# Two-layer decoder on one core: in the last entry's attention with heads of 64, the routed rows' transposes and the first piece of the shared expert go ahead of the denominators' last sums

## The chip, the cores and the metric

The kernel runs on one core of one Trainium2 chip. The metric is the device time of one execution in microseconds (us), the median of several runs. Five runs of the kernel before gave 1140.53 to 1144.34 us, median 1142.88.

The engines are named as the profile names them: PE is TensorE (matmuls and transposes), PEld its weight loads, DVE is VectorE, ACT ScalarE, POOL GpSimd, and SP the SyncE queue that issues most DMAs.

## The reference, cut to what matters

The program is a decoder of two layers on `x` of 8 entries by 256 tokens by 256 dimensions, all in float32. Layer 0 has self-attention, cross-attention and a routed feed-forward part; layer 1 has causal self-attention, cross-attention with 16 heads of 64, and experts. The change lies where the last two meet:

```python
# L1 cross-attention, context (8, 256, 512), one null key and value in front
q = q * scale
sim = jnp.einsum('bhid,bhjd->bhij', q, k)
attn = jax.nn.softmax(sim, axis=-1)
out = jnp.einsum('bhij,bhjd->bhid', attn, v)
out = jnp.einsum('bnf,fd->bnd', out, Wout)
out = layernorm(out) * ln_scale + ln_bias
...
# L1 experts: one of 8 per token, and a shared one for all tokens
x_aD = layernorm(x).reshape(2048, 256)
scores_aE = x_aD @ router_DE              # the best expert's score gives the gate
shared_aD = jax.nn.silu(x_aD @ ws1_DF) * (x_aD @ ws3_DF) @ ws2_FD     # F = 704
```

The softmax needs, per head and query, the sum of the exponentials over the keys (the denominator). The shared expert needs nothing but the normalized rows of the tokens that it is applied to.

## The kernel before, in words

**The cross-attention with heads of 64** (`null_cross_attention`) is a loop over the 8 entries. The 16 heads stand as 8 pairs `c`; a pair's 128 rows are its two heads of 64. For each pair, `weighted` (called once per entry) does the following:

- TensorE makes the scores `stx` of both heads and both halves of the keys (line 1554), ScalarE their exponentials `pTx` (line 1558), and GpSimd adds the two halves of the keys into `both` (line 1560).
- TensorE multiplies exponentials and values into `ox` (line 1594), two pairs to a PSUM tile. The result goes to `oT` in SBUF, undivided, by ScalarE for pairs 0, 1, 4, 5 and by VectorE for pairs 2, 3, 6, 7 (line 1602).
- `sums` (line 1569) sums `both` over its partitions with a small matmul against a column of ones, `hot8`, into one PSUM tile `den` of 128 by 256, two matmuls per pair. The sums of a block of two pairs are issued one block later; those of the last block, pairs 6 and 7, are left to `rest()`, which the loop calls where it likes.

Then `reciprocals` (lines 1611 to 1636) adds the null key's exponential `en` to `den` and takes the reciprocal `r` on VectorE (lines 1614 and 1615). It sends `r` to DRAM as `rd` with four DMAs on SP (line 1621) and back as `rs`, spread over 64 partitions each, with two more (line 1625). Beside that, GpSimd forms `en * r`, and two VectorE operations test the range of `r` (lines 1631, 1632). `divide` (line 1649) multiplies `oT` by `rs` in four parts of two pairs; in the last entry GpSimd does the first and third, VectorE the second and fourth. `outward` (line 1653) makes the product with `Wout` in seven smaller products (the tiles `wo` and `woz`) from blocks of `oT` and their sums and differences `swo` (lines 1463 to 1466, VectorE), then norms the result and adds it to `x`. Between its sixth and its seventh product it runs one step of other work, `between`.

**What fills the gap in the last entry.** In the first seven entries the next entry's keys, values and queries are made while `rs` is under way. The last entry has no next one, so pieces of the shared expert take their place. `hidden_shared(0, ...)` (lines 1191 to 1200, over `hidden`, line 1178) is a generator over six pieces of the first quarter of the tokens (512 of 2048, entries 0 and 1). A whole piece is four matmuls of 128 by 128 by 512 into a pair of PSUM banks `hx` (line 1196), which the profile shows as eight rows, each matmul of the program twice; then a silu on ScalarE into `spx` (line 1188) and a product with the other bank on VectorE into `mid` (line 1189). The sixth piece is a half one. The pairs for `hx` come from a pool with two buffers. Four pieces run between the reciprocals and `divide`, the fifth within `outward`, the sixth behind it.

In the same place stand the routed rows: `routed_rows(b - 1, ...)` (line 1316) transposes the normalized rows of entry 6 with four TensorE transposes (line 287, tile `tr`, three PSUM buffers shared with `ox`) into `xnTe`, copied by ScalarE; `routed_scores(b - 1)` (line 1331) makes their router scores `sc` behind the first piece.

**What sets the order.** From the point where `order.enter_context(tc.manual_schedule(...PE...))` stands, TensorE runs in the order in which the program is written. The other engines' queues are put in order by the framework's scheduler, from its own estimate of when things are ready. Every engine then works through its queue in order and waits on semaphores.

So the last entry's order on TensorE is: last `ox`, last `den` sums, `tr`, piece 1, `sc`, pieces 2 to 4, `outward`. On VectorE, ahead of the last two copies of `ox`, stand sums of the shared weights (`tws`, line 1208) and of rows (`sx`, lines 1220 to 1223); behind the copies come `rx` and its reciprocal, the two range tests, the copy of `sc`, three `mid` products, the two divides, the first `swo` sum, the fourth `mid` product and the other `swo` sums.

Of the kernel before, what the change touches and what calls it, by code (L numbers as in the profile page):

```python
# [157 lines left out]
def plain(  # L158
# [101 lines left out]
    def layernorm_T(b, work, mm, bufs=2):  # L260

        xn = work.tile([P, 2, D], F32, tag="xn", name="xn", bufs=bufs)
        mv, rs = norm_stats([x[:, 2 * b + t, :] for t in range(2)], 1e-5, small, "ln")
        for t in range(2):
            last = normed(xn[:, t, :], x[:, 2 * b + t, :], mv, rs, t)
        return last, transposed(xn, work, mm, "xnT", bufs=bufs)
# [308 lines left out]
    first = ExitStack()  # L575
# [315 lines left out]
    def context(b):  # L891
        t = ctxs.tile([P, CTX // P, S], F32, tag="ctxT", name="ctxT")
        nc.sync.dma_start(t, a["ctx_T"][b].rearrange("(c p) t -> p c t", p=P))
        return t

    def key_room():
        return kvs.tile([P, nc8, S], F32, tag="kT", name="kTx")
# [280 lines left out]
    def hidden(mid, first, n, pair, silu):  # L1178

        for i in range(NFC):  # L1180
            h1, h3 = pair(n)
            for h, lo in ((h1, i * P), (h3, FF + tail + i * P))[: 2 if i < full else 1]:
                first(h, lo)
            fw = P
            if i == full:
                fw, h1, h3 = tail, h1[:tail], h1[tail:]
            sl = silu(n)[:fw]
            nc.scalar.activation(sl, h1, AF.Silu)  # L1188
            yield nc.vector.tensor_tensor(mid[:fw, i, :n], sl, h3, ALU.mult)  # L1189

    def hidden_shared(q, pair, silu):


        def first(h, lo):
            for c in range(2):
                nc.tensor.matmul(
                    h, shared["ws13"][:, c, lo : lo + P], shared["xnT"][:, c, bass.ts(q, 2 * S)], start=c == 0, stop=c == 1
                )

        return hidden(shared["mid_s"][q % 2], first, 2 * S, pair, silu)  # L1200
# [105 lines left out]
    def routed_norm(b, work):  # L1306

        xn = work.tile([P, 2, D], F32, tag="y", name="xne", bufs=1)
        mv, rs = norm_stats([x[:, 2 * b + t, :] for t in range(2)], 1e-5, small, "ln")
        for kept, v in zip(norms[b], (mv, rs)):  # L1310
            nc.gpsimd.tensor_copy(kept, v)
        for t in range(2):
            normed(xn[:, t, :], x[:, 2 * b + t, :], mv, rs, t)
        return xn

    def routed_rows(b, xn, work):
        if b < B - 2:
            rows_of[b] = transposed(xn, work, mm, "xnk", bufs=1)
            nc.sync.dma_start(xt[b], rows_of[b])
        else:  # L1320
            rows_of[b] = transposed(xn, work, mm, "", shared["xnT"][:, :, bass.ts(b, S)])
# [87 lines left out]
    def null_cross_attention(phase):  # L1409
# [44 lines left out]
        def sums_of_rows(rows, n, name, apart, pool=wsum):  # L1454


            def block(i, j):
                return rows[:, n * j : n * (j + 1), bass.ts(i, P)]

            sw = pool.tile([P, 4 if apart else 3, n, P], F32, tag=name, name=name, bufs=1)  # L1460
            s1, s2, s4 = (sw[:, i] for i in range(3))
            s3 = sw[:, 3] if apart else block(1, 0)
            nc.vector.tensor_tensor(s1, block(1, 0), block(1, 1), ALU.add)
            nc.vector.tensor_tensor(s2, s1, block(0, 0), ALU.subtract)
            nc.vector.tensor_tensor(s4, block(0, 1), s2, ALU.subtract)
            nc.vector.tensor_tensor(s3, block(0, 0), block(1, 0), ALU.subtract)
            return block(0, 0), block(0, 1), s4, block(1, 1), s1, s2, s3
# [143 lines left out]
        def reciprocals(b, den, en):  # L1611

            r = work.tile([P, S], F32, tag="rx", name="rx", bufs=1)
            nc.vector.tensor_tensor(r, den, en, ALU.add)
            nc.vector.reciprocal(r, r)
            rd = dram.tile([2, nc8, S], F32, name=f"rd{b}")
            rs = work.tile([P, nc8, S], F32, tag="rs", name="rs", bufs=1)
            for g in range(2):
                for i in range(2):
                    at = XD * g + HP * i  # L1620
                    nc.sync.dma_start(
                        rd[g].rearrange("(c i) q -> i c q", i=2)[i], r[at : at + nc8 // 2, :]
                    )
            for g in range(2):
                nc.sync.dma_start(
                    rs[XD * g : XD * (g + 1)].rearrange("p c q -> p (c q)"),
                    rd[g : g + 1].rearrange("g c q -> g (c q)").to_broadcast([XD, nc8 * S]),
                )
            nc.gpsimd.tensor_tensor(en, en, r, ALU.mult)
            low = work.tile([P, S], F32, tag="low", name="low", bufs=1)  # L1630
            nc.vector.tensor_scalar(low, r, 1.0e-25, None, ALU.is_ge)
            nc.vector.scalar_tensor_tensor(
                low, r, 1.0e25, low, ALU.is_le, ALU.mult, accum_out=fit[:, b : b + 1]
            )
            return rs
# [75 lines left out]
        def spare():  # L1711
            return work.tile([P, 2, 2 * S], F32, tag="pT", name="spx", bufs=4)
# [20 lines left out]
        for b in range(B):  # L1733
            more = b + 1 < B
            if more:
                ctxT = context(b + 1)
            oT, den, rest = weighted(kT, v, qT)
            if more:
                _, xnT = layernorm_T(b + 1, work, mm, 1)
                if b:  # L1740
                    xe = routed_norm(b - 1, work)
                of_ctx = sums_of_rows(ctxT, CTX // P // 2, "sw", False)
            else:
                xe = routed_norm(b - 1, work)
                rest()

                wproj.close()
                late = ctx.enter_context(tc.tile_pool(name="late", bufs=1, side="right"))
                load_shared(late, lambda: ctx.enter_context(tc.tile_pool(name="mids", bufs=1, side="right")))
                tables = ctx.enter_context(tc.tile_pool(name="route", bufs=1, side="right"))  # L1750
                sums = phase.enter_context(tc.tile_pool(name="sums", bufs=1, side="right"))
                order.enter_context(tc.manual_schedule(engines={mybir.EngineType.PE}))
            if more:
                order.enter_context(tc.manual_schedule(engines={mybir.EngineType.PE}))
            if b:
                routed_rows(b - 1, xe, work)
            if more:
                of_x = sums_of_rows(xnT, 1, "swq", True)
                kT, v, qT = key_room(), value_room(), query_room()
                k7 = seven("k7", of_ctx, w_terms(kv_blocks, 0), kT, False)  # L1760
                v7 = seven("v7", of_ctx, w_terms(kv_blocks, 1), v, True)
                q7 = seven("q7", of_x, w_terms(q_blocks, 0), qT, False)
                next(k7)
                rest()
            rs, old = reciprocals(b, den, en), en
            if not b:
                sums_of_weights(o_blocks, slice(0, 4))
            if b == 1:
                in_range()
            if not more:  # L1770
                w_out(shared["ws2"], a["L1_ffn_ws2_FD"])
                routing_tables(tables)
            if more:

                for made in (k7, k7, v7, k7, k7, k7, v7, v7, q7, v7, q7, v7, v7, q7):
                    next(made)
            else:
                first = hidden_shared(0, pair, lambda n: spare()[:, 0, :n])
                for i in range(4):
                    next(first)  # L1780
                    if i == 0:
                        routed_scores(b - 1)
                shared["of_w"] = sums_of_shared(*(sums.tile([P, full * P], F32, name=f"tws{i}") for i in range(4)))
            divide(oT, rs, (nc.gpsimd, nc.gpsimd if more else nc.vector))
            outward(b, oT, old, lambda: next(q7 if more else first))
            if more:
                next(q7)
                if b:
                    routed_scores(b - 1)
                next(q7)  # L1790
                en = null_key(xnT)
            else:
                for _ in first:
                    pass
            order.close()
# [1230 lines left out]
```

## Time and profile before, and how to read it

| | before |
|---|---|
| median of 5 runs | 1142.88 us (1140.53 to 1144.34) |
| profiled execution, its own time | 1144.87 us |
| its span, first to last instruction | 1143.1 us |
| TensorE matmuls busy | 1093.1 us, 96% |
| TensorE weight loads busy | 715.8 us, 63% |
| VectorE, ScalarE, GpSimd busy | 52%, 40%, 38% |
| mean granted TensorE clock | 0.990 |
| last entry's end of attention | about 855 to 897 us of the span |

The trace has, for every instruction, its start, its duration, and the idle time of its engine just before it, with the engine, the tile and the line that ended that idle time. A row of the timeline can merge several like instructions; the count at its end says how many, and its duration then runs from the first start to the last end. Matmul ends are modelled, and rows on GpSimd are rough. The granted clock is the share of TensorE's full speed that its throttle allowed.

### The profile page before, as it was taken

Reading aid. Unit: us, or ns where it says so; the run is one execution under the profiler, and the core shown is the slowest. Engines: PE = TensorE matmul, PEld = TensorE weight load, DVE = VectorE, ACT = ScalarE, POOL = GpSimd, SP = SyncE. Lnnn points to the kernel's source line nnn. Section 1 sums busy time; section 2 is a strip of 40 time slices with the busy share of each in tenths; the row PEclk is TensorE's granted clock in tenths of the full one; section 3 lists DMA queues with packets and bytes.
Section 4 is the critical chain, followed back from the end, with each engine's and each line's share of the span. In section 5 each row is a group of like instructions: output and inputs, shape, how many; then the busy total and the mean of one; then the engine's idle time right before and its main releaser. Section 6 shows DMA issues by size and latency. Waiting matters only on the chain. (4 is left out here: it accounts for less than half of the span.)

```text
span 1143.1 us, 34931 instructions
## 1 busy us (share of the span) xinstructions
PE 1093.1 (96%) x15186; PEld 715.8 (63%) x15186; DVE 591.6 (52%) x1573; ACT 460.9 (40%) x747; POOL 439.4 (38%) x519
## 2 busy tenths in 40 slices
PE   6999999989899999999999999999999999999996
PEld 3444545544544545777777777777775768888864
DVE  5576776778686628344434352525257672222213
ACT  4776766665454533232323232323233321322220
POOL 2456364547587623433242424242425133000023
PEclk9999999999899999999999999999999999999999
DMA  8048344134033400101010101010122045999924
GB/s 261 5 159 283 100 133 124 58 124 133 30 124 102 187 2 20 39 20 48 20 49 20 48 20 48 20 48 20 48 103 69 1 159 200 369 414 397 372 70 128
DMA packets 62819, 130.87 MB, mean 114 GB/s; under 512 B 9904, under 2 KB 45984, under 8 KB 58304
## 3 DMA queue, kind: packets, MB, share of 16 engines
q1 hardware_dynamic: 54944, 108.61, 27.9%
q0 software_dynamic: 4992, 16.92, 4.1%
q10 hardware_dynamic: 2720, 3.02, 0.8%
q8 instruction: 121, 1.98, 0.7%
q14 instruction: 42, 0.34, 0.1%
HBM read 110.03 MB, written 35.80 MB: 128 GB/s over the span
## 5 line engine op out<-in xcount | busy, mean ns | idle before, releaser
L341 ACT ACTIVATE pT<-st 128x1024 f32<-128x1024 f32 (+1 forms) x128 | 110.5, 916 | 64.7 <-PE st L330 58.8
L367 PE MATMUL o<-pT,padv 128*32 128x256 f32 (+1 forms) x1536 | 96.6, 367 | 1.6 <-DVE by_q L383 1.1
L1560 POOL TENSOR_TENSOR both<-pTx 128x512 f32<-128x512 f32 x64 | 87.4, 1395 | 21.0 <-ACT pTx L1558 19.1
L272 PE MATMUL h<-xrT,w 128*64 128x128 f32 (+1 forms) x1936 | 87.1, 250 | 0.7 <-issue 0.7
L272 PEld LDWEIGHTS h<-xrT,w 128*64 128x64 f32 x1936 | 84.5, 137 | 3.7 <-issue 1.3
L341 ACT ACTIVATE pT<-st,kbias 128x1024 f32<-128x1024 f32 x64 | 67.9, 1113 | 36.8 <-PE st L330 34.8
L1189 DVE TENSOR_TENSOR midr<-sl,h 128x128 f32<-128x128 f32 x102 | 29.4, 288 | 101.3 <-PE h L272 68.8
L367 PEld LDWEIGHTS o<-pT,padv 128*32 128x32 f32 x1536 | 44.6, 110 | 53.4 <-issue 23.8
L1558 ACT ACTIVATE pTx<-stx 128x1024 f32<-128x1024 f32 x64 | 62.5, 1024 | 31.4 <-PE stx L1554 28.1
L1188 ACT ACTIVATE sl<-h 128x128 f32<-128x128 f32 (+1 forms) x114 | 35.4, 311 | 94.9 <-PE h L272 55.9
L330 PE MATMUL st<-qm,kT 32*128 32x512 f32 (+1 forms) x512 | 68.6, 594 | 4.9 <-ACT qm L309 1.9
L278 PE MATMUL qk<-xnT,l_wqkv 128*32 128x256 f32 x1024 | 69.0, 396 | 0.6 <-issue 0.6
L1554 PE MATMUL stx<-qTx,kTx 64*128 64x256 f32 x512 | 64.4, 391 | 2.1 <-ACT pTx L1558 2.1
L1594 PE MATMUL ox<-pTx,vx 128*32 128x256 f32 x1024 | 63.3, 380 | 0.0
L383 DVE STREAM_TRANSPOSE by_q<-o 128x512 f32<-128x512 f32 x48 | 34.1, 710 | 51.2 <-PE o L367 51.1
L1649 POOL TENSOR_TENSOR oT<-oT,rs 128x512 f32<-128x512 f32 x30 | 37.2, 1271 | 60.3 <-DMA rs<-rd 60.3
L1554 PEld LDWEIGHTS stx<-qTx,kTx 64*128 64x128 f32 x512 | 46.1, 186 | 20.4 <-issue 7.0
L346 POOL TENSOR_SCALAR_AFFINE_SELECT pT<-pT 128x512 f32<-128x512 f32 x64 | 41.9, 672 | 35.6 <-ACT pT L341 34.9
L254 POOL TENSOR_TENSOR lxrs<-lxve,mhalf 128x2 f32<-128x2 f32 x8 | 5.7, 706 | 129.4 <-DVE lxve L252 129.4
L278 PEld LDWEIGHTS qk<-xnT,l_wqkv 128*32 128x32 f32 x1024 | 34.2, 114 | 28.8 <-issue 9.3
L2014 PE MATMUL out<-w,midr 128*64 128x256 f32 x408 | 47.6, 379 | 1.0 <-issue 1.0
L1594 PEld LDWEIGHTS ox<-pTx,vx 128*32 128x32 f32 x1024 | 35.3, 110 | 21.1 <-issue 2.7
(397 smaller groups left out, 2225.3 us busy)
## 6 DMA issues: line engine op xcount, KB each, us to landing
w<-packs SPq DMA_DIRECT2D x22, 1408.0 KB
w<-packs SPq DMA_DIRECT2D x22, 768.0 KB
rs<-rd SPq DMA_DIRECT2D x16, 512.0 KB
packs<-L_ffn_w_eDF SPq DMA_DIRECT2D x8, 704.0 KB
packs<-L_ffn_w_eDF SPq DMA_DIRECT2D x8, 640.0 KB
packs<-L_ffn_w_eFD SPq DMA_DIRECT2D x8, 640.0 KB
ctxT<-ctx_T SPq DMA_DIRECT2D x8, 512.0 KB
wkv_x<-L_xattn_Wkv POOLq DMA_DIRECT2D x1, 4096.0 KB
```

Source lines behind the costliest of these rows:

```text
L272: nc.tensor.matmul(out[h], lhsT[:, h], rhs, start=start, stop=stop, skip_group_check=True)
L278: nc.tensor.matmul(out[h : h + HP], lhsT[:, h : h + HP], rhs, start=start, stop=stop, skip_group_check=True)
L330: nc.tensor.matmul(st[:, r, :, :n], self.kT[rows, c, bass.ts(kt, P)], self.qm[rows, :, c, q0:], start=True, stop=True,)
L341: nc.scalar.activation(pT[:, :, :, :n], st[:, 2 * k : 2 * k + 2, :, :n], AF.Exp, scale=self.scale, **kb)
L346: nc.gpsimd.affine_select(out=pT[:, :, :, :P], in_=pT[:, :, :, :P], compare_op=ALU.is_ge, fill=0.0, base=0, pattern=[[0, 2], [0, 2], [1, P ...
L367: nc.tensor.matmul(o[HP * j : HP * j + HP, m, q0:], self.v_pad[:, kt, 8 * c + 2 * j + m, :], pTs[j // 2][:, j % 2, m, : S - q0], start=kt ...
L1554: nc.tensor.matmul(st[:, g, kt, :], kT[rows, c, bass.ts(kt, P)], qT[rows, c, :], start=True, stop=True)
L1558: nc.scalar.activation(pT, st, AF.Exp, scale=scale)
L1560: nc.gpsimd.tensor_tensor(both, pT[:, :, 0, :], pT[:, :, 1, :], ALU.add)
L1594: nc.tensor.matmul(o[at : at + HP, i, :], v[:, kt, 2 * (c2 + i) + g, lo : lo + HP], pT[:, g, kt, :], start=kt == 0, stop=kt == 1, skip_gro ...
L1649: engines[c2 % 4 // 2].tensor_tensor(oT[:, c2 : c2 + 2, :], oT[:, c2 : c2 + 2, :], rs[:, c2 : c2 + 2, :], ALU.mult)
L2014: nc.tensor.matmul(ps[h], mid[:, i, h], sets[k % len(sets)][1][:, i, :], start=i == 0, stop=i == NFC - 1, skip_group_check=True,)
```

## The change

In the last entry, `rest()` (the sums of pairs 6 and 7) moves from ahead of the closing of pools and the loads of the shared expert's weights to behind the routed rows' transposes and behind the first step of `hidden_shared`. The generator is therefore made earlier, and the later loop takes three steps of it instead of four; `routed_scores` stands behind the first of these, which is now the second piece. Nothing else of the program differs; the pools, the loads and the arithmetic are the same.

```diff
@@ -1742,7 +1742,6 @@
                 of_ctx = sums_of_rows(ctxT, CTX // P // 2, "sw", False)
             else:
                 xe = routed_norm(b - 1, work)
-                rest()
 
                 wproj.close()
                 late = ctx.enter_context(tc.tile_pool(name="late", bufs=1, side="right"))
@@ -1762,6 +1761,10 @@
                 q7 = seven("q7", of_x, w_terms(q_blocks, 0), qT, False)
                 next(k7)
                 rest()
+            if not more:
+                first = hidden_shared(0, pair, lambda n: spare()[:, 0, :n])
+                next(first)
+                rest()
             rs, old = reciprocals(b, den, en), en
             if not b:
                 sums_of_weights(o_blocks, slice(0, 4))
@@ -1775,8 +1778,7 @@
                 for made in (k7, k7, v7, k7, k7, k7, v7, v7, q7, v7, q7, v7, v7, q7):
                     next(made)
             else:
-                first = hidden_shared(0, pair, lambda n: spare()[:, 0, :n])
-                for i in range(4):
+                for i in range(3):
                     next(first)
                     if i == 0:
                         routed_scores(b - 1)
```

## The prediction

> **What bounds the kernel now.** I read the page first. Its busy row says that TensorE's matmuls fill the span, so a step is worth what it does to TensorE's own queue, and any moment in which TensorE stands still behind 868 us is paid in full unless a later stall swallows it.
>
> ```profile
> PE 1093.1 (96%) x15186; PEld 715.8 (63%) x15186; DVE 591.6 (52%) x1573; ACT 460.9 (40%) x747; POOL 439.4 (38%) x519
> ```
>
> The chain of waits on the page is no help: it holds three pieces of the last microsecond. So I went on to the list of waits, for TensorE alone. From 889 us to the end it stood still five times, 0.2 to 1.0 us each, 3.1 us in all, and each time for another engine that had itself been fed by TensorE (or for nothing that shows). None of these is a wait for something with a clock of its own, so nothing behind the place of the change gives a delay back.
>
> Then the timeline of the place itself. Columns: start, duration, engine, line and operation, count, and in brackets the idle time before and who ended it.
>
> ```profile
> 867.11 0.39 PE L1594 MATMUL ox<-pTx,vx 128*32 128x256 f32 x2
> ...
> 867.98 0.62 PE L1569 MATMUL den<-both,hot 128*32 128x256 f32 x4 [0.45 <-POOL both L1560]
> 868.12 1.27 DVE L1602 COPY oT<-ox 128x512 f32<-128x512 f32 x2
> 868.86 0.66 PE L287 MATMUL tr<-ident,xne 128*128 128x128 f32 x4 [0.26 <-DVE oT L1602]
> 869.32 0.41 DVE L1614 TENSOR_TENSOR rx<-den,en 128x256 f32<-128x256 f32 x1
> 869.35 3.60 PE L1196 MATMUL hx<-xnTe,ws 128*128 128x512 f32 x8
> 869.77 1.75 DVE L1615 RECIPROCAL rx<-rx 128x256 f32<-128x256 f32 x1
> ...
> 872.88 0.64 PE L272 MATMUL sc<-router,xnTe 128*64 128x8 f32 x16
> ...
> 873.45 10.57 PE L1196 MATMUL hx<-xnTe,ws 128*128 128x512 f32 x24
> ...
> 880.59 2.49 POOL L1649 TENSOR_TENSOR oT<-oT,rs 128x512 f32<-128x512 f32 x2 [7.57 <-DMA rs<-rd]
> 881.92 2.31 DVE L1649 TENSOR_TENSOR oT<-oT,rs 128x512 f32<-128x512 f32 x2
> ...
> 883.95 1.09 PE L272 MATMUL wo<-wout_x,oT 128*64 128x128 f32 x16
> ```
>
> The reader is to see two things. TensorE stands still around the last `den` sums twice, 0.45 us for GpSimd's last `both` and 0.26 us for VectorE's late copy of `ox`, 0.71 us together. And from those sums a second chain runs: `rx`, reciprocal, out to DRAM and back, divide, outward product. That chain comes home just in time: VectorE's first divide ends near 883.6 (it began at 881.92; the two of them take 0.68 and 1.71 us by their rows), and the product `wo` that needs it starts at 883.95, directly behind the last `hx`. The margin is about 0.3 us, and four pieces of the shared expert, 14 us, are what covers the chain.
>
> **The change, part by part.** No instruction is added or removed; in the built streams only the queues of TensorE and VectorE change their order, those of ScalarE, GpSimd and SP do not. TensorE's `den` matmuls move behind the four transposes and the first piece. VectorE's first `mid` product moves ahead of the two range tests, and the fourth moves ahead of the divides.
>
> *The stall in front.* The transposes do not come sooner: they write the PSUM buffer that VectorE's first late copy frees (868.12 + 0.63 = 868.75), and the copies stand behind the weight sums in VectorE's queue, which the change leaves alone. So `tr` starts at 868.86 as before and TensorE is idle from 867.52 (867.12 + 0.40, the end of what runs with the last `ox`) to there, 1.34 us. The sums, which lay inside that wait, now cost their own time behind the first piece: two full rounds of eight rows, at 858.34 and 862.57, each held TensorE 0.46 and 0.45 us until the next product. So **+0.46 us** (below 0.3 seems excluded, the rows being real work; 0.7 if the change of tile form costs something, though `hx` to `sc` and back shows no gap). What was meant to fill a wait fills none, since another wait of the same length lay behind it.
>
> *The chain behind.* One piece takes 872.88 - 869.35 = 3.53 us, so `den` now starts at 872.88. `rx` followed the start of `den` by 0.70 to 0.71 us in four earlier entries (466.64 to 467.35, 523.87 to 524.57, 581.63 to 582.34, 754.95 to 755.65), so it starts at 873.58 instead of 869.32, 4.26 us later. VectorE idles meanwhile; behind `rx` wait only the `mid` products, whose PSUM pairs are needed again two pieces later. Sum and reciprocal end 2.20 us on, at 875.78. From the reciprocal's end to GpSimd's first divide the eight entries show 8.53 to 9.76 us, this one 9.07: SP's six DMAs (four out, two back, nothing queued behind them there) are the same. The first divide can start at 884.85 and ends at 886.12 (1.27 us).
>
> *TensorE's side.* It reaches `wo` at 883.95 + 0.46 = 884.41, behind three pieces instead of four since `den`. VectorE must first do the fourth `mid`: silu starts 0.17 us after the matmuls (884.12 against 883.95) and takes 0.60, the product follows 0.03 us later with 0.69, so VectorE is free at 885.90. Its first divide then waits for GpSimd's running one, as VectorE's 881.92 row did in before (1.71 us beside GpSimd's second, 0.68 alone): 886.12 + 0.69 = 886.8. `wo` starts near 886.9 instead of 884.41. GpSimd's second divide runs 886.8 to 888.05, VectorE's second to 888.65, and the second half of `woz`, in before at 885.31 (884.87 plus half of 0.88), starts at 888.7: 3.4 us late. The sums `swo` behind it keep ahead of their products. With the longest of the eight round trips it is 4.1 us, with the shortest VectorE comes second to GpSimd and it is still 3.5; if VectorE got its turn at once, 2.9. I take **+3.4 us in all, the 0.46 included**: about 3.0 us of standing still, 2.5 of it in one piece.
>
> *The clock.* Between its first and its last matmul the kernel runs at full granted clock but for four times before 302 us. Cut at the edges of those times, the span falls into a raster of 3.41 us. Columns: stretch, its length, busy time of PE, PEld, DVE, ACT, POOL, the granted clock, DMA.
>
> ```profile
> 168.07:171.48 3.41, 1.67 (x15) 1.06 (x16) 3.17 (x8) 1.41 (x3) 0.06 (x1) 1.00 0.61 222
> 171.48:174.90 3.42, 3.42 (x28) 1.08 (x28) 0.00 (x0) 2.12 (x3) 1.21 (x1) 0.50 0.02 5
> ...
> 277.30:280.71 3.41, 1.83 (x19) 0.91 (x12) 3.34 (x7) 0.59 (x1) 3.22 (x4) 1.00 0.62 224
> 280.71:284.12 3.41, 3.41 (x24) 1.24 (x25) 1.47 (x7) 1.91 (x3) 1.76 (x3) 0.50 0.23 82
> 366.04:369.46 3.42, 1.95 (x36) 1.07 (x32) 3.35 (x6) 1.37 (x3) 2.65 (x4) 1.00 0.34 61
> 369.46:372.87 3.41, 3.41 (x57) 1.62 (x56) 3.38 (x12) 1.94 (x2) 2.17 (x4) 1.00 0.97 394
> 434.31:437.72 3.41, 1.90 (x18) 1.10 (x16) 3.41 (x14) 1.17 (x2) 0.00 (x0) 1.00 0.45 137
> 437.72:441.14 3.42, 3.42 (x36) 2.27 (x34) 3.42 (x7) 1.17 (x2) 0.00 (x0) 1.00 0.07 21
> ```
>
> Subtract PE's busy time from the length. A raster stretch with 1.58 us idle or more (1.58, 1.74, and two others with 1.94 and 2.05) is followed by one at half clock, one with 1.47 or 1.51 is not. A stall of 2.5 us in one piece puts at least 1.58 us into one stretch unless the raster cuts it nearly in the middle, which I work out as some 5 to 10% of positions. The next 3.41 us then run at half clock, and since outward product and shared expert behind it are bound by TensorE, that costs half of 3.41, **+1.7 us**; nothing if the raster lies well, 3.4 if a second stretch follows, as it did once (6.8 us at 294.3). I take 1.7. The stall in front, 1.34 us, stays below the mark.
>
> The Trainium skill speaks against this term: "TensorE: Matmul & The Clock Gate", Part 1, has the clock fall to half only after at least one idle window of about 3.4 us. By that rule a 3 us stall is free of it and the sum stays at +3.4 us; by the rows above, where 1.58 us was enough, it is 5.1. The measurement decides.
>
> **The sum**: 3.4 + 1.7 = +5.1 us. The profiled execution took 1144.87 us (span 1143.1 and 1.8 around it), so one like it would take 1150.0. It lies 2.0 us above the median of 1142.88, and I put the sum on the median: **1148.0 us**.
>
> **Rivals.**
> *The stall comes, the clock stays up* (the raster cuts the stall, or what is granted follows something other than idle time): 1142.9 + 3.4 = 1146.3 us.
> *The clock falls twice*, since the 1.34 us in front reach the mark with a little more idle time, or since the stall spans two stretches: 5.1 + 1.7, 1149.7 us.
> *The chain is mostly covered*, because the round trip is quicker with nothing else on the queues: then little but the 0.46 us of the sums remains, 0.5 to 2 us, say 1144.0. Against it: the trip varied by 1.2 us in eight entries, and the fourth `mid` alone holds VectorE until 885.9.
> *Faster.* The mechanism: the transposes wait for VectorE's copy in name only, and go at 867.52 once the sums no longer stand ahead of them. TensorE then gains 1.34 us and pays 0.46, and the chain starts 1.34 us sooner too; the gain of 0.9 us, 1142.0, stays only if the divides are done when `wo` is reached, near 883.1. They would be done near 885.5, so it decides at a round trip of about 6.7 us, against the 8.53 to 9.76 measured. That excludes it but for an error in my reading.
> *That the change does nothing* is ruled out by the built queues: `den` stands between the two pieces.
>
> **How the numbers follow.** Forecast 0.66, clock stays up 0.14, clock falls twice 0.08, covered 0.08, faster 0.04. Some 0.2% of 1142.88, 2.3 us, is about what a measurement of this kernel can tell from no change. The first three lie above it but for a few hundredths of noise: slower 0.86, same 0.10, faster 0.04. The range runs from 1145.0 (a short stall at full clock, 2.9 us, and 0.8 of noise below) to 1150.4 (4.1 us, 1.7 and noise, or two falls); outside are faster, most of covered, and a tail above.
>
> **What would show it.** In the changed kernel's timeline: `tr` still released by VectorE's copy after 1.3 us of idle time; `den` near 872.9; `rx` near 873.6; GpSimd's first divide near 885; `wo` 2 to 3 us idle behind `oT`; and a stretch of half clock within 4 us of it. If `tr` starts at 867.6, or `wo` follows `hx` without a gap, I am wrong; if the granted clock stays at 1.00 behind 880 us, the last 1.7 us are.

## The result, and the profile after

The changed kernel takes **1145.87 us** (median of 35 runs, 1141.47 to 1150.17), the kernel before 1141.28 us in the same measurement (61 runs, 1135.57 to 1145.80). The ratio is 1.0039 with a 95% interval of 1.0030 to 1.0048, so the change costs 4.5 us (3.4 to 5.5). The prediction was 5.1 us more.

The page of the changed kernel hides this. Its profiled execution took 1145.52 us with a span of 1143.7 us, only 0.6 us more than the span before, and TensorE's busy time is even lower:

```profile
PE 1087.6 (95%) x15186; PEld 714.8 (62%) x15186; DVE 591.6 (52%) x1573; ACT 460.4 (40%) x747; POOL 438.8 (38%) x519
```

TensorE's 5.5 us are not less work, for the count is the same. In the execution of before the granted clock had fallen four times before 302 us (five stretches of 3.41 us at half clock), in that of after once (two such stretches, from 288.77 us). So the last `ox` product ended at 867.50 us in before and at 863.91 us in after, 3.6 us earlier, ahead of anything that the change touches. Two single spans therefore can't be compared. What can is the **section** from the end of the last `ox` to the first matmul of the second quarter of the shared expert (line 1237): the same work in each kernel, with the change inside it. Before it took 867.50 to 896.92, 29.42 us; after, 863.91 to 896.78, 32.87 us: **+3.45 us**, at full clock on both sides. From there to the end of the span it was 246.2 and 246.9 us, so nothing was given back.

The place itself, from the timeline of after (the same view as that of before in the prediction, and the same columns: start, duration, engine, line and operation, count, idle time before and who ended it). To set a time beside one of before, add 3.59 us:

```profile
861.82 2.09 PE L1594 MATMUL ox<-pTx,vx 128*32 128x256 f32 x30
...
864.55 1.27 DVE L1602 COPY oT<-ox 128x512 f32<-128x512 f32 x2
...
865.29 0.66 PE L287 MATMUL tr<-ident,xne 128*128 128x128 f32 x4 [1.37 <-DVE oT L1602]
...
869.31 0.64 PE L1569 MATMUL den<-both,hot 128*32 128x256 f32 x8
...
869.88 3.70 PE L1196 MATMUL hx<-xnTe,ws 128*128 128x512 f32 x8
...
870.07 0.42 DVE L1614 TENSOR_TENSOR rx<-den,en 128x256 f32<-128x256 f32 x1 [4.24 <-issue]
870.53 1.75 DVE L1615 RECIPROCAL rx<-rx 128x256 f32<-128x256 f32 x1
...
881.15 2.49 POOL L1649 TENSOR_TENSOR oT<-oT,rs 128x512 f32<-128x512 f32 x2 [7.52 <-DMA rs<-rd]
...
882.47 0.66 PE L272 MATMUL wo<-wout_x,oT 128*64 128x128 f32 x8 [1.26 <-POOL oT L1649]
882.54 2.25 DVE L1649 TENSOR_TENSOR oT<-oT,rs 128x512 f32<-128x512 f32 x2
...
884.24 0.66 PE L272 MATMUL wo<-wout_x,oT 128*64 128x128 f32 x8 [1.11 <-DVE oT L1649]
...
884.73 1.04 PE L272 MATMUL woz<-wout_x,oT 128*64 128x128 f32 x16
...
896.78 1.03 PE L1237 MATMUL hx<-xnTe,ws 128*128 128x256 f32 x4
```

The rows of before that stand beside the last two:

```profile
884.87 1.04 PE L272 MATMUL woz<-wout_x,oT 128*64 128x128 f32 x16
...
896.92 1.03 PE L1237 MATMUL hx<-xnTe,ws 128*128 128x256 f32 x4
```

The reader is to see three things. The transposes still wait for VectorE's copy, in one piece of 1.37 us where before it was 0.45 and 0.26 around the sums. The sums now stand between two pieces of the shared expert, and `rx` comes 0.76 us behind them. And `wo`, which in before ran through without a gap (one row of 16), is cut in two: its first eight rows wait 1.26 us for GpSimd's divide, the other eight 1.11 us for VectorE's.

Where the 3.45 us come from is read by counting from the end of `ox` in both. `tr` is late by 0.02 us. The sums cost 0.57 us until the next `hx`, and the piece behind them takes 3.63 instead of 3.53 us: 0.67 in all. `wo` waits 1.26 us and starts 1.39 late against its work; between the starts of `wo` and `woz` lie 2.26 instead of 0.92 us, of which 1.11 are the wait. The idle figures thus tell 2.37 of the 2.73 us that the two breaks cost; the other 0.36 go where rows no longer overlap their neighbours, twice. The 0.03 that remain are within what the rows can tell.

The granted clock around the stall, in stretches of the same raster (columns as in the prediction: stretch, length, busy PE, PEld, DVE, ACT, POOL, granted clock, DMA):

```profile
879.28:882.69 3.41, 2.15 (x9) 0.79 (x9) 0.76 (x2) 0.60 (x1) 1.54 (x2) 1.00 0.10 19
882.69:886.10 3.41, 2.29 (x42) 2.05 (x40) 3.27 (x4) 0.27 (x1) 0.95 (x1) 1.00 0.00 0
886.10:889.52 3.42, 3.42 (x67) 3.42 (x64) 1.94 (x6) 0.53 (x2) 0.00 (x0) 1.00 0.00 0
```

The raster cut the stall in two, 1.26 and 1.12 us idle, both short of the mark, and the clock stayed up. In this execution the clock term of the prediction is missing.

### The profile page after: what moved, and what is told of

The parts are those of the page before. It is cut to its first block, busy times and chain, and to the rows that moved or that the text cites. A ratio compares the mean times of both kernels' runs of the same rounds, so it can differ in the third digit from the quotient of the medians.

```text
span 1143.7 us, 34931 instructions
## 1 busy us (share of the span) xinstructions
PE 1087.6 (95%) x15186; PEld 714.8 (62%) x15186; DVE 591.6 (52%) x1573; ACT 460.4 (40%) x747; POOL 438.8 (38%) x519
```

## The experiments

The theory tested, **A**, is the prediction's: the late sums cost their own time, gain nothing in front because VectorE's copy holds the transposes anyway, and delay the chain through reciprocal, DRAM and divides, so that the outward product waits. **B** has the loss arise where the sums stand, in the middle of the shared expert's matmuls, and not from the late chain. **C** is the clock term: a stretch with more than about 1.6 us idle is followed by one at half clock. **D** denies it: the clock falls only after a whole idle stretch. **E** has the transposes held by something other than VectorE's copy.

The times below are sections as defined above, from one profile each; the section of before is 29.42 us, of after 32.87 us. Ratios of the median times are to the kernel before on the same chip, with 95% intervals. The kernel before had a median of 1129.35 us on the chip of the first four kernels and of 1142.25 us on that of the next four, so times of different groups are not compared.

### One part alone, and the cover given back

**rows_only**: of the change, only the transposes go ahead of the sums.

```diff
                 next(k7)
                 rest()
             if not more:
+                rest()
                 first = hidden_shared(0, pair, lambda n: spare()[:, 0, :n])
                 next(first)
-                rest()
```

> Measure: from the end of the last ox to the first matmul of the second quarter (line 1237), 29.4 us in before and 32.9 us in after. Theory A (what costs is that the chain behind the sums starts one piece later and comes home after TensorE has run out of work): the sums start some 1.3 us later than in before, not 5, and TensorE itself comes 0.5 us later, so the chain is home in time: +0.5 us (0.3 to 1.0), no wait at wo, time within 0.1% of before. Rival B (the sums cost so much because they no longer lie in TensorE's wait and change the tile form in mid-stream): most of the 3.5 us is there already, 32 us or more, time about +0.3%.

Section 30.18 us, +0.76; 1130.79 us, ratio 1.0012 (0.9994 to 1.0030). The transposes waited 1.36 us for VectorE's copy, the sums followed them, and `wo` ran through with no wait. Moving the sums behind the transposes alone costs about their own time.

**piece_only**: the first piece and the sums go ahead of the routed rows.

```diff
-            if b:
+            if b and more:
                 routed_rows(b - 1, xe, work)
...
                 next(first)
                 rest()
+                routed_rows(b - 1, xe, work)
```

> The piece fills the wait for the last both and for VectorE's copy, so TensorE gains 0.7 us in front; the sums start 3.1 us later than in before. Theory A: GpSimd's first divide 2.5 us later than in before counted from the last ox, wo waits some 2 us, section +1.8 us (1.2 to 2.4), between before and after, and a fall of the clock is rarer than in after. Rival B: the sums are in mid-stream as in after, but nothing is lost in front: about +0.5 us or a gain.

Section 31.20 us, +1.78; 1131.72 us, ratio 1.0012 (0.9993 to 1.0031). The piece starts at once behind `ox`, so the 1.36 us in front are gone; the sums' time and the two waits at `wo` (1.04 for GpSimd, 1.12 for VectorE) remain. The clock did not fall.

**fifth_piece**: the change as it is, with a fifth piece ahead of the outward product.

```diff
-                for i in range(3):
+                for i in range(4):
```

> The changed kernel with the fifth piece ahead of the outward product instead of within it (the half piece takes its place there), so that four pieces stand between the sums and wo as in before. Theory A: TensorE reaches wo at about +4.0 us, the divides are done, no wait: section +0.5 us (0.3 to 1.2), clock full behind 860 us, time within 0.15% of before and 0.3% or more below after. Rival B: the sums stand where they stand in after, so +3.4 us stay.

Section 30.08 us, +0.66; 1131.03 us, ratio 1.0011 (0.9995 to 1.0028). TensorE's rows in its timeline:

```profile
862.02 0.64 PE L1569 MATMUL den<-both,hot 128*32 128x256 f32 x8
...
866.79 10.57 PE L1196 MATMUL hx<-xnTe,ws 128*128 128x512 f32 x24
877.29 1.09 PE L272 MATMUL wo<-wout_x,oT 128*64 128x128 f32 x16
```

The sums stand as late as in the changed kernel, but three pieces follow `sc` instead of two, and `wo` is one row of 16 again with no wait. Only the sums' 0.66 us are left. This is the experiment that parts A from B: B falls, and of the 3.45 us some 2.8 are the uncovered chain.

**after_again**: the changed kernel once more, on this chip; no edit.

> The changed kernel as it is, for another position of the clock's raster. Section +3.4 us at full clock (3.2 to 4.2). Theory C (a raster stretch of 3.41 us with 1.57 us or more idle is followed by one at half clock): the wait at wo is in two parts of 1.3 and 1.1 us with 0.7 of work between, so 0.58 of all positions bring 1.57 us into one stretch; then a stretch of half clock follows and the section is 1.5 to 1.7 us longer. Rival D (a stall shorter than a whole stretch leaves the clock alone): never. Mean by C: 3.4 + 0.58 x 1.7 = 4.4 us, by D 3.4 us.

Section 34.52 us, +5.10; 1134.44 us (11 runs), ratio 1.0042 (1.0024 to 1.0061). The waits at `wo` are 1.24 and 1.12 us as before, but this time both fall into one stretch:

```profile
869.38:872.79 3.41, 1.06 (x15) 0.78 (x16) 2.65 (x3) 0.60 (x1) 2.45 (x2) 1.00 0.00 0
872.79:876.21 3.41, 3.41 (x36) 3.41 (x34) 2.97 (x6) 0.27 (x1) 0.00 (x0) 0.50 0.00 0
876.21:879.62 3.41, 3.41 (x66) 3.33 (x62) 0.57 (x2) 0.53 (x2) 0.00 (x0) 1.00 0.03 5
```

Of 3.41 us, 2.35 were idle, and the next stretch ran at half clock: the 16 rows of `woz` took 1.93 us there instead of 1.04. Against the 32.87 us of the profile above that is 1.65 us more, C's price. D falls: two waits of 1.2 us in one stretch were enough.

### The wait in front, and the margin behind

**copies_act**: the change, with VectorE's two copies of `ox` in the last entry given to ScalarE.

```diff
-        def weighted(kT, v, qT):
+        def weighted(kT, v, qT, last=False):
...
-                (nc.vector.tensor_copy if c2 % 4 else nc.scalar.copy)(oT[:, c2 : c2 + 2, :], o)
+                (nc.vector.tensor_copy if c2 % 4 and not last else nc.scalar.copy)(oT[:, c2 : c2 + 2, :], o)
...
-            oT, den, rest = weighted(kT, v, qT)
+            oT, den, rest = weighted(kT, v, qT, not more)
```

> The changed kernel with all four copies of ox in the last entry on ScalarE, which is idle there, so that the transposes' PSUM buffer is free when the last ox ends. Theory A: the 1.36 us of idle time in front of tr go (to 0.1), everything behind keeps its distances: section (end of the last ox to the first matmul of the second quarter) 32.9 - 1.3 = 31.6 us at full clock (31.2 to 32.0), the two waits at wo as in after, 1.2 and 1.1 us; 1.6 us more if a stretch of half clock follows them. Rival E (the wait in front isn't VectorE's copy but something that the sums had hidden): tr still waits over 1 us, section 32.9.

Section 31.33 us, +1.91 over before and 1.54 under after; 1144.53 us, ratio 1.0029 (1.0010 to 1.0048). In its timeline:

```profile
862.03 0.66 PE L287 MATMUL tr<-ident,xne 128*128 128x128 f32 x4
862.52 3.60 PE L1196 MATMUL hx<-xnTe,ws 128*128 128x512 f32 x8
866.05 0.64 PE L1569 MATMUL den<-both,hot 128*32 128x256 f32 x8
```

The last `ox` ended at 862.10, and the transposes follow it without a gap. So what held them was VectorE's copy, as the prediction read it, and E falls. The two waits at `wo` stay (1.16 and 1.12 us), since the sums and all that hangs on them came sooner by as much as TensorE's work did.

**rows_act**: the edits of rows_only and copies_act together.

```diff
-                (nc.vector.tensor_copy if c2 % 4 else nc.scalar.copy)(oT[:, c2 : c2 + 2, :], o)
+                (nc.vector.tensor_copy if c2 % 4 and not last else nc.scalar.copy)(oT[:, c2 : c2 + 2, :], o)
...
             if not more:
+                rest()
                 first = hidden_shared(0, pair, lambda n: spare()[:, 0, :n])
                 next(first)
-                rest()
```

> Only the transposes ahead of the sums (rows_only: section 30.2 us), and the copies on ScalarE as in copies_act. Theory A: tr lies in the wait for the last both, the sums start 0.6 us behind the last ox and no longer wait, TensorE loses neither of the two waits of before and pays the sums' 0.6 us in full: section 28.8 to 29.2 us against 29.42 in before, no wait at wo; time 0.2 to 0.6 us below before, which the times can't tell from no change. Rival E: as rows_only, 30.2 us.

Section 28.76 us, 0.66 less than before, with no wait at `wo`; 1142.51 us, ratio 1.0005 (0.9989 to 1.0022). Here the transposes do fill the time in which the last `both` is awaited. The section shows the gain; the time can't be told from that of before.

**less_cover**: the change with one piece less ahead of the outward product.

```diff
-                for i in range(3):
+                for i in range(2):
```

> The changed kernel with the fourth piece behind the outward product's sixth product and the fifth behind its seventh, so two pieces instead of three stand between the sums and wo. Theory A: wo still starts when the divides allow it, 18.6 us behind the last ox, TensorE waits 4.8 us and some 0.5 to 1.1 more for VectorE, and the piece left out comes later: section 32.9 + 3.0 = 35.9 us at full clock (35.4 to 36.6). Theory C: more than 1.8 us of idle time in a raster stretch at every position, so half clock follows always, once or twice: 1.6 to 3.3 us more, section 37 to 39.5. Rival D (only a whole idle stretch of 3.41 us does it): at 4.8 us in 4 of 10 positions.

Section 37.22 us, +7.80; 1149.11 us (four runs), ratio 1.0080 (1.0048 to 1.0111). Its timeline:

```profile
883.91 1.97 PE L272 MATMUL wo<-wout_x,oT 128*64 128x128 f32 x16 [5.35 <-POOL oT L1649]
885.67 1.82 PE L272 MATMUL woz<-wout_x,oT 128*64 128x128 f32 x16
```

With the cover 3.5 us shorter, the wait becomes 5.35 us, one piece, and the products behind it run at half clock (`woz` 1.82 us). The less cover, the more is lost: 0.66 us with a fifth piece ahead, 3.45 with four, 7.80 with three, clock included. Here one stretch was idle throughout (880.43 to 883.84 us) and the fall came behind it, while the 1.86 us idle in the stretch before it brought none. So this run doesn't part C from D. C's section, 37 to 39.5 us, was met, but its premise that more than 1.8 us idle always bring a fall did not hold for that stretch.

**one_matmul**: the sums behind the first of the piece's four matmuls, the routed rows behind the piece. (The added lines move later line numbers by four in its profile.)

```diff
-    def hidden_shared(q, pair, silu):
+    def hidden_shared(q, pair, silu, at=0, do=None):
...
+        made = []
...
-                nc.tensor.matmul(
+                made.append(nc.tensor.matmul(
...
-                )
+                ))
+                if len(made) == at:
+                    do()
...
-            if b:
+            if b and more:
...
-                first = hidden_shared(0, pair, lambda n: spare()[:, 0, :n])
+                first = hidden_shared(0, pair, lambda n: spare()[:, 0, :n], 1, rest)
                 next(first)
-                rest()
+                routed_rows(b - 1, xe, work)
```

> One matmul of the first piece (0.88 us) ahead of the sums, the other three and then the transposes behind them: something that waits for nothing lies in the wait for the last both, and the transposes come when VectorE's copy is done. Theory A: the sums start 0.9 us behind the last ox instead of 0.5, rx still waits for VectorE's own copies, so the chain is no later; neither of the two waits of before is left and the sums cost 0.6 us in full: section 29.0 us (28.7 to 29.4), no wait at wo, 0.3 us at a product of the swo sums at most. Time 0 to 0.7 us below before, not to be told from no change. Rival B (sums in mid-stream cost more than their own time): 30 us or more.

Section 29.04 us, 0.38 less than before; 1141.22 us, ratio 1.0000 (0.9985 to 1.0014). One matmul of the program (two rows) writes to a PSUM pair that is free, so it does not wait for VectorE's copy, and it fills the wait for `both`; the sums follow 0.98 us behind `ox`, soon enough that `wo` has no wait:

```profile
865.11 1.13 PE L1198 MATMUL hx<-xnTe,ws 128*128 128x512 f32 x2
866.16 0.64 PE L1573 MATMUL den<-both,hot 128*32 128x256 f32 x8
...
881.01 1.09 PE L272 MATMUL wo<-wout_x,oT 128*64 128x128 f32 x16
```

### How often the clock falls

**look_1**, **look_2** and **look_3** are the changed kernel, unedited, one execution each.

> The changed kernel once more, for the position of the clock's raster alone. From the profiles so far: a raster stretch with 1.88 us or more idle was always followed by half clock, one with 1.53 or less never. The wait at wo (1.26 us, 0.66 of work, 1.11) then brings half clock in 0.45 to 0.58 of all positions; section 32.9 us without it, 34.5 with it.

> The changed kernel once more, as in look_1: section 32.9 us where the raster cuts the wait so that no stretch has 1.6 us idle, 34.5 us where one has 1.9 or more; between these the profiles leave it open.

> The changed kernel once more, as in look_1: section 32.9 us where the raster cuts the wait so that no stretch has 1.6 us idle, 34.5 us where one has 1.9 or more; between these the profiles leave it open.

| | section us | over before | waits at `wo`, us | most idle in one stretch | half clock behind |
|---|---|---|---|---|---|
| after | 32.87 | +3.45 | 1.26, 1.11 | 1.26 | no |
| after_again | 34.52 | +5.10 | 1.24, 1.12 | 2.35 | yes |
| look_1 | 33.22 | +3.80 | 1.83, 0.47 | 1.68 | no |
| look_2 | 32.93 | +3.51 | 1.33, 1.11 | 1.33 | no |
| look_3 | 33.02 | +3.60 | 1.40, 1.12 | 1.43 | no |

The clock fell in one of five. The mean of the five sections is +3.9 us, of the four at full clock +3.6; the measured +4.5 (3.4 to 5.5) holds both. How often the clock falls behind this stall is not settled by five executions: with these waits and a mark between 1.57 and 1.88 us it would be 0.40 to 0.58 of the raster's positions, an estimate that one in five does not refute. That it falls nearly always is unlikely: the mean granted clock was 0.9952 over the 11 timed runs of after_again and 0.9949 over the 34 of before beside them (single runs scatter by 0.0017), where a fall in every run would take off 0.0015 (half of 3.41 us of 1131). Whether the clock accounts for what lies between 3.6 and 4.5 us stays open.

## Why the prediction was right, and where it was not

Counted from the end of `ox`, step by step:

- **The transposes do not come sooner.** Right: 1.37 us idle against 1.34, and copies_act shows the copy as the cause by taking it away.
- **The sums' own time.** 0.67 us against 0.46, near the bound of 0.7 that was kept for a change of tile form. The rows in before, which were taken as the price, stand in a stream of products of the same 128 by 32 form. Here the sums stand between matmuls of 128 by 128: 0.57 us for themselves and 0.10 for the piece behind them. That the form is the reason was not tried by itself. fifth_piece, where nothing else is left, gives 0.66.
- **The chain.** `den` at +5.40 us (predicted +5.38), `rx` 0.76 us later (0.70), from the reciprocal's end to GpSimd's first divide 8.87 us (9.07).
- **The wait at the outward product.** Its end was right, its shape wrong. `woz` stands at +20.82 us instead of +17.37, 3.45 late, and 3.4 was predicted for its second half. But the prediction had `wo` wait once, 2.5 us, for VectorE's first divide, which it gave 0.69 us and a turn between GpSimd's two. In fact the first half of `wo` needs GpSimd's first divide alone, and started behind it. So the margin in before was misread too: VectorE's first divide ended at 883.63 us (881.92 + 1.71), and the second half of `wo`, which needs it, began near 884.4. That is 0.8 us and not 0.3. And the turn was missed by little: VectorE's fourth `mid` ended at 882.62 us (881.93 + 0.69), 0.2 us after GpSimd's first divide (881.15 + 1.26 = 882.41), where the prediction had it 0.2 us before. So GpSimd's second divide went on at 882.38, and VectorE's first, begun at 882.54, took 1.65 us beside it. In look_1, whose round trip was longer (9.45 us), `mid` was done first and VectorE got its turn: its divide took 1.00 us, `wo` had one wait, and `woz` a second one for GpSimd.
- **The clock, +1.7 us taken as nearly sure. This is the step that failed.** "A stall of 2.5 us in one piece puts at least 1.58 us into one stretch unless the raster cuts it nearly in the middle": it is not in one piece. Two waits of 1.26 and 1.11 us with 0.66 us of work between them span 3.0 us, so the raster's edge often falls between them or inside one. And for one piece of 2.5 us the working was off: an edge leaves less than 1.58 us on both sides if it falls between 0.92 and 1.58 us into the stall, 0.66 of 3.41 us, which is 19% of positions and not 5 to 10. The price, when it fell, was 1.65 us. Its chance was worked out as over 0.9 (the chances at the end give 0.74 against 0.14); it was seen once in five.
- **The sum.** It was met because the measured 4.5 us lie between the sums without a fall, 3.4, and with one, 5.1. As far as the clock term goes that is luck: at one fall in five it is worth 0.3 us and not 1.7, and the mean section of +3.9 us doesn't explain all of the 4.5.

Of the rivals, "the stall comes, the clock stays up" is what four of five executions did. "Mostly covered" is refuted by the waits; what it expected comes about only with a fifth piece. "Faster" failed where it was said to, at the copy; and even without the copy, in copies_act, the kernel is slower, since its round trip, 8.8 us, is not the 6.7 that it needed.

## What to carry to other kernels

When work is moved ahead of an instruction to fill a wait, look for a second wait behind the first: here the moved transposes needed a copy that came no sooner than what they were to cover. Before delaying the head of a long chain through other engines and DRAM, read the margin at its far end; here 0.8 us of margin stood against 4.3 us of delay, and the smallest step that filled the gap (one matmul, in one_matmul) cost nothing behind. And compare the section in which the change lies, since two spans of the same kernel differ by more than the change is worth.

## What the runs showed of the hardware

The clock falls sooner than after a stretch without any work. Over the thirteen profiles of this case, between first and last matmul, every full-clock stretch of 3.41 us with 1.88 us idle or more was followed by half clock (23 of 23), none with 1.53 us or less, and of those between 1.57 and 1.87 us 8 of 19; the prediction's mark of 1.58 lies at the lower edge of a mixed band. "TensorE: Matmul & The Clock Gate", Part 1, of the Trainium skill, which the prediction set against its clock term, has the fall come after at least one idle window of about 3.4 us; in after_again 2.35 us idle in a stretch of 3.41 us were enough. The measurement decides: the window need not be idle throughout.

Two divides on GpSimd and VectorE at once are hardly quicker than one after the other: VectorE's took 1.65 us beside GpSimd's of 1.27 and 0.68 alone. The pair took 1.81 us (882.38 to 884.19), one after the other it would be 1.95. What in the chip holds them apart was not tried.

An idle figure understates a break in a stream of matmuls: the two breaks at `wo` cost 2.73 us where the rows show 2.37 us idle.
